# Keys of the second attention held in a zero-filled tile of four row blocks per sequence

## The chip, the cores and the metric

The kernel runs on one NeuronCore of a Trainium2 chip. The metric is device time in microseconds (us): three runs of the kernel before took 1682.60, 1684.46 and 1688.49, median 1684.46. In the profile the core's engines are PE (TensorE's matmuls) with PEld (its weight loads), DVE (VectorE), ACT (ScalarE), POOL (GpSimd) and SP (SyncE, here the issuer of DMAs).

## The reference, cut to what matters

Two decoder layers on `x` of 32 sequences x 128 positions x 256 features, in f32: six sublayers, each added to `x`. The change lies in the fifth, the second layer's cross attention:

```python
def _L1_xattn_ref(q, k, v, Wq, bq, Wk, bk, Wv, bv):
    NUM_HEADS = 16
    B, S, D = q.shape                     # 32, 128, 256
    H, hd = NUM_HEADS, D // NUM_HEADS     # 16, 16
    qp = (q @ Wq + bq).reshape(B, H, S, hd)
    kp = k @ Wk + bk                      # one set of keys for all heads
    vp = v @ Wv + bv
    att = jnp.einsum('bhsd,btd->bhst', qp, kp) / math.sqrt(D)
    att = jax.nn.softmax(att, axis=-1)
    out = jnp.einsum('bhst,btd->bhsd', att, vp)
    return out.transpose(0, 2, 1, 3).reshape(B, S, D)
```

Here `q` is the layer-normed `x`, `k` and `v` are `ctx_1024`. Each of the 16 heads has only 16 features, and all heads of a sequence share the same 128 keys.

## The kernel before

**Stages.** The sublayers run one after another: A (first attention, to about 200 us), B (retention-like cross attention, to about 560), C (experts, to about 1010), D (the rotation sublayer), E (the attention above), F (routed experts, to the end). Stage B also makes the keys and values of stage E, for all groups, and keeps them in SBUF. D, E and the routing of F are interleaved: `stage_e` works in steps `b`, one sequence per step, from b = -13 to 32. E's own scores run from 1138 to 1468 us of the profile.

**Layout.** Sequences come in 8 groups of 4 (`GB = 4`). `kp[g]` has 128 rows and 4 x 128 columns. Its rows are four equal copies (row blocks of 32) of the same keys: 16 rows of key features, one row of ones, 15 rows of zeros. The queries `qT` are 128 rows (four heads of 32 rows: 16 features and 16 zeros) x 4 blocks `j` x 4 sequences x 128 queries. So head 4j + r is block j, row block r.

**Two scores.** The softmax needs the maximum of each query's scores, along the free axis, and then the exponentials with keys on the partitions, for the product with the values. The scores are therefore computed twice:

- `largest` (L1468): for each block j and row block r, queries as weights, keys as moving data, 32 rows, 128 x 128 out. 16 matmuls a sequence. They fill four PSUM banks, one per r, with j inside the bank. Four reductions on DVE (L1475), one per bank, write minus the maximum into a padded tile, `e_pad`.
- `less` (L1481, L1483): four transposes of `e_pad` and an addition on DVE put minus the maximum into the queries' free row, opposite the keys' row of ones. The result is `e_qm`.
- `scores` (L1490): keys as weights, `e_qm` as moving data, 32 rows x 512 columns, one matmul per row block r, each into its own bank. ACT takes the exponential of each bank (L1491).
- `values` (L1498) and `back` (L1508 to L1520): product with the values, transposes, division by the sum, and the addition to `x` on POOL.

**Order.** PE's instructions run in the order in which they are written (`manual_schedule`). In step b it is: `largest` of sequence b+1; `queries` and `turn` of a coming group (L1450, L239); parts of D's rotation (L1296, L1332, L1354) and of F's routing (L156, L354, L355, L611, L629, L633); `values` of b-1; `scores` of b; `back` of b-1; `less` of b+1. The other engines' orders, SP's too, are set by a scheduler. [...]

**Buffers.** PSUM is eight banks: four with the tag "s" (both scores) and four with the tag "m" (all else). `e_hT` (normed, transposed input of a group) and `e_qm` have two buffers each.

**SP in this stage.** Before the change, SP issues here D's writes of `d_line` (L1224), its reads of `d_om` (L1284, in `Turned`, one a group), and, once D's tiles are free, the weights of F's experts (L1628, two loads of 1 MB and a small one). After them come the reads of F's expert blocks (L441).

Of the kernel before, what the change touches and what calls it, by code (L numbers as in the profile page):

```python
# [22 lines left out]
F32 = mybir.dt.float32  # L23
I32 = mybir.dt.int32
AF = mybir.ActivationFunctionType
ALU = mybir.AluOpType
AX = mybir.AxisListType

P = 128
B = 32  # L30
D = 256
NC = D // P
GB = 4
NG = B // GB
GT = GB * P
H = 16
HD = 16
# [3 lines left out]
OM = 64  # L41
# [450 lines left out]
class Route:  # L492


    name = "c"
# [48 lines left out]
class RouteF(Route):  # L544


    name = "f"
# [729 lines left out]
class Turned:  # L1277


    def __init__(self, lie, g, pool):  # L1280
        self.lie, self.k, self.nc, self.g, self.pool = lie, lie.k, lie.nc, g, pool
        self.om = self.full("om")
        half, first = divmod(g * GB, B // 2)
        self.nc.sync.dma_start(out=self.om[0:OM], in_=lie.line[half][first : first + GB].rearrange("b i j -> i b j"))  # L1284

    def tile(self, shape, name, **kw):
        return self.pool.tile(shape, F32, name=f"d_{name}", **kw)
# [123 lines left out]
def stage_e(k, lie, p1, dram, right, halves):  # L1411


    nc, tc = k.nc, k.tc
    J = R = 4
    with (
# [6 lines left out]
        for i in range(2):  # L1423
            t = p1.tile([P, H, 2 * HD], F32, name=f"e_pad{i}")
            nc.gpsimd.memset(t, 0.0)
            pads.append(t)

        k.cf = p1.tile([P, NG, GB, 32], F32, name="f_cf")
        nc.gpsimd.memset(k.cf, 0.0)
        nc.gpsimd.memset(k.cf[:, :, :, E : E + 1], 1.0)  # L1430

        class Group:


            def __init__(self, g):
                self.g = g
                self.stats = k.stats(g)
                self.hT = p2.tile([P, NC, GT], F32, name="e_hT")
                self.qT = p2.tile([P, J, GB, P], F32, name="e_qT")

            def norm(self, behind=None):
# [5 lines left out]
            def queries(self, j, first=0, n=GB):  # L1447
# [7 lines left out]
                    self.qT[:, j, first : first + n], pq, AF.Identity, bias=k.col("E_bq", j)  # L1455
                )

        class Seq:
            def __init__(self, group, i):
                self.group, self.g, self.i = group, group.g, i  # L1460
                self.keys = k.kp[group.g][:, i * P : (i + 1) * P]

            def largest(self):
                ps = [k.bank([P, J, P], "s") for _ in range(R)]
                for j in range(J):
                    for r in range(R):
                        rows = slice(32 * r, 32 * r + 32)
                        nc.tensor.matmul(  # L1468
                            ps[r][:, j, :], lhsT=self.group.qT[rows, j, self.i, :], rhs=self.keys[rows, :],
                            start=True, stop=True,  # L1470
                        )
                self.pad = pads[self.i % 2]
                slots = self.pad.rearrange("p (j r) d -> p j r d", r=R)
                for r in range(R):
                    nc.vector.tensor_reduce(slots[:, :, r, HD], ps[r], AX.X, ALU.max, negate=True)  # L1475

            def less(self):
                pm = k.bank([P, J, P])
                flat = self.pad.rearrange("p m d -> p (m d)")
                for j in range(J):  # L1480
                    nc.tensor.transpose(pm[:, j, :], flat[:, j * P : (j + 1) * P], k.ident)  # L1481
                self.qm = p2.tile([P, J, P], F32, name="e_qm")
                self.less_by = nc.vector.tensor_add(self.qm, pm, self.group.qT[:, :, self.i, :]).ins  # L1483

            def scores(self):
                self.e = p2.tile([P, R, J, P], F32, name="e_e")
                for r in range(R):
                    rows = slice(32 * r, 32 * r + 32)
                    ps = k.bank([P, J, P], "s")
                    nc.tensor.matmul(ps, lhsT=self.keys[rows, :], rhs=self.qm[rows], start=True, stop=True)  # L1490
                    self.exp_by = nc.scalar.activation(self.e[:, r], ps, AF.Exp, scale=1.0 / 16.0).ins  # L1491

            def values(self):
# [28 lines left out]
        with tc.manual_schedule(engines={mybir.EngineType.PE}):  # L1522
            groups, seqs, routes, turned = {}, {}, {}, {}

            def seq(b):
                if 0 <= b < B and b not in seqs:
                    seqs[b] = Seq(groups[b // GB], b % GB)
                return seqs.get(b)

            def step(b, rest=iter(())):  # L1530
                g, i = divmod(b, GB)
                before, this, nxt = seq(b - 1), seq(b), seq(b + 1)

                def due(of, n):

                    lag, rest = divmod(b - n, GB)
                    return of.get(lag) if rest == 0 else None

                route = lambda n: due(routes, n)
                if nxt:  # L1540
                    nxt.largest()
                for n in (-4, -3):
                    if q := due(groups, n):
                        if q.g:
                            for j in range(2 * n + 8, 2 * n + 10):
                                q.queries(j)
                        else:
                            for j in range(J):
                                q.queries(j, 2 * n + 8, 2)
                if q := due(groups, -5):  # L1550
                    q.turn()
                for n, what in ((-9, "add"), (-10, "spin"), (-11, "cube"), (-12, "head"), (-12, "square")):
                    if t := due(turned, n):
                        getattr(t, what)()
                next(rest, None)
                for n, half in ((9, 0), (10, 1)):
                    if r := route(n):
                        r.choose(half)
                if r := route(7):
                    r.turn()  # L1560

                if g == NG - 1:
                    r = routes[i // 2]
                    if i % 2 == 0:
                        r.hidden()
                        r.turn_shares()
                    else:
                        r.shared()
                if before:
                    before.values()  # L1570
                if r := route(12):
                    r.place()
                if this:
                    this.scores()
                if before:
                    before.back()
                if nxt:
                    nxt.less()


                less_by = nxt.less_by if nxt else None
                exp_by = this.exp_by if this else None
                if b >= 5 and i == 1:
                    routes[g - 1] = RouteF(k, g - 1, halves[(g - 1) * 2 // NG], pf, less_by)
                if i == 3 and g + 4 < NG:
                    turned[g + 4] = Turned(lie, g + 4, pd)
                    turned[g + 4].norm(exp_by)
                if i == 1 and 0 <= g + 2 < NG:
                    groups[g + 2] = Group(g + 2)
                if q := due(groups, -6):  # L1590
                    q.norm(exp_by)
                if r := route(6):
                    r.norm(exp_by)
                if r := route(11):
                    r.rank(less_by)
                if r := route(12):
                    r.share(less_by)
                lag, rest = divmod(b - 13, GB)
                if lag in routes:
                    last = routes[lag].store(rest, before.summed)  # L1600
                    if rest == 0:
                        routes[lag].root(last)
                if b == B - 5:
                    halves[0].finish()

            with tc.tile_pool(name="dw", bufs=1, side="right") as pool:
                lie.operands(pd)
                rest = stage_d(k, lie, pool, dram, p2)
                for b in range(-13, -1):
                    step(b, rest)  # L1610
            pf = right.enter_context(tc.tile_pool(name="f1", bufs=2, side="right"))
            for b in range(-1, B + 1):
                if b == B - 12:

                    turns.close()
                    experts = Experts(k, right.enter_context(tc.tile_pool(name="f2", bufs=1, side="right")))
                step(b)
# [185 lines left out]
def sublayers(ctx, k):  # L1803
# [35 lines left out]
    halves = [Dispatch(k, f"g{n}", n * B // 2, B // 2, p1, p2) for n in range(2)]  # L1839
    right = ctx.enter_context(ExitStack())  # L1840
    stage_f(k, *stage_e(k, lie, e1, pd, right, halves), halves)


# [125 lines left out]
```

## Time and profile before

| | us |
|---|---|
| median of three runs | 1684.46 |
| profiled execution, whole | 1686.57 |
| profiled execution, span | 1684.5 |
| PE busy in the span | 1483.5 |
| PEld busy | 982.6 |
| DVE busy | 930.6 |
| ACT busy | 605.6 |
| POOL busy | 601.8 |

How to read the profile: a row of a group names line, engine, operation, the tiles it writes and reads, the shapes and the number of instructions; then busy time in us and the mean length of one instruction in ns; then how long the engine sat idle just before such instructions and what ended that wait. The length of a matmul is its latency: matmuls are pipelined, so the group's busy time and the distance between starts tell the cost. PE's clock is granted in shares of full speed; the mean over the span is 0.926. Stage E's rows in the page:

```profile
L1475 DVE TENSOR_REDUCE e_pad<-ps 128x4 f32<-128x512 f32 x128 | 82.4, 683 | 13.6 <-PE ps L1468 8.9
L1491 ACT ACTIVATE e_e<-ps 128x512 f32<-128x512 f32 x128 | 67.3, 604 | 28.4 <-PE ps L1490 28.3
```

### The profile page before, as it was taken

How to read it: one execution, taken by the hardware profiler on the slowest of the kernel's cores; microseconds unless marked ns; L12 is line 12 of the kernel's file. 1: busy time of each engine (PE TensorE's matmuls, PEld its weight loads, DVE VectorE, ACT ScalarE, POOL GpSimd, SP SyncE). 2: the span in 40 equal slices, each digit the busy share in tenths (PEclk: the TensorE clock that was granted, in tenths of full speed). 3: DMA queues.
4: the chain of work that ended last, by engine and by line, in shares of the span. 5: the costliest groups of instructions: out<-in, count | busy, mean ns of one | idle time of the engine just before them, and what ended most of it. 6: DMA issues, size and time to landing. Idle time of an engine off the chain costs nothing.

```text
span 1684.5 us, 26942 instructions
## 1 busy us (share of the span) xinstructions
PE 1483.5 (88%) x9233; PEld 982.6 (58%) x9233; DVE 930.6 (55%) x3005; ACT 605.6 (36%) x1542; POOL 601.8 (36%) x621
## 2 busy tenths in 40 slices
PE   6999799999997499999999995799999998878873
PEld 3555577776675356666666664445555554556662
DVE  7565446777777533333333324546667766554575
ACT  2444333333333022222222221156665554433331
POOL 2111036577768611111111113122324433365552
PEclk9999999999999589999999995789999988788997
DMA  9990299911002821111111108000000110043486
GB/s 336 336 336 27 68 305 305 254 40 36 24 27 97 330 59 47 47 45 45 48 48 45 45 22 317 12 6 6 3 2 20 66 37 26 26 129 111 141 271 221
DMA packets 133257, 183.85 MB, mean 109 GB/s; under 512 B 12059, under 2 KB 113253, under 8 KB 131077
## 3 DMA queue, kind: packets, MB, share of 16 engines
q1 hardware_dynamic: 116500, 142.28, 27.4%
q0 software_dynamic: 13296, 36.52, 5.9%
q10 hardware_dynamic: 3328, 3.33, 0.6%
q8 instruction: 77, 1.26, 0.3%
q14 instruction: 56, 0.45, 0.1%
HBM read 69.80 MB, written 112.30 MB: 108 GB/s over the span
## 4 chain that ended last, share of the span: by engine, by line
PE 70%; DVE 12%; issue 5%; ACT 5%; POOL 4%; DMA 3%; another core or an unknown queue 1%; POOLq 0%; SPq 0%; ACTq 0%; DVEq 0%
PE ps L1066 13%; PE ps L1086 7%; PE ps L156 6%; PE ps L664 3%; PE ps L1490 2%; PE ps L1450 2%; PE ps L1468 2%; PE ps L1674 2%; PE ps L1690 2%; PE ps L881 2%; PE ps L239 2%; PE ps L1079 2%; PE ps L151 2%; PE ps L897 2%; PE ps L840 1%
## 5 line engine op out<-in xcount | busy, mean ns | idle before, releaser
L1066 PE MATMUL ps<-c_up,c_xT 128*128 x568 | 269.0, 597 | 0.0
L342 POOL DMA_INDIRECT r_ys<-c_yb,r_toi x71 | 68.1, 959 | 354.1 <-DVE r_w L460 313.8
L1066 PEld LDWEIGHTS ps<-c_up,c_xT 128*128 128x128 f32 x568 | 103.2, 192 | 74.0 <-issue 69.7
L1086 PE MATMUL ps<-c_down,c_hid 128*128 x568 | 134.8, 380 | 0.9 <-DVE c_hid L1081 0.9
L1086 PEld LDWEIGHTS ps<-c_down,c_hid 128*128 128x128 f32 x568 | 107.4, 190 | 47.2 <-issue 17.9
L887 DVE TENSOR_TENSOR b_sim<-ps,b_decay 128x512 f32<-128x512 f32 x128 | 79.6, 683 | 83.6 <-PE ps L881 50.9
L146 POOL TENSOR_TENSOR b_rs<-b_var,mhalf 128x16 f32<-128x16 f32 x32 | 93.5, 2922 | 83.8 <-DVE b_var L915 80.7
L1091 ACT ACTIVATE c_yb<-ps,r_w 128x256 f32<-128x256 f32 x71 | 33.6, 473 | 219.0 <-PE ps L1086 219.0
L1081 DVE COPY c_hid<-ps 128x512 f32<-128x512 f32 x71 | 49.1, 691 | 101.5 <-PE ps L1079 101.5
L342 POOL DMA_INDIRECT g_ys<-f_yb,g_toi x78 | 75.7, 971 | 65.0 <-DVE g_to L447 49.3
L1475 DVE TENSOR_REDUCE e_pad<-ps 128x4 f32<-128x512 f32 x128 | 82.4, 683 | 13.6 <-PE ps L1468 8.9
L146 POOL TENSOR_TENSOR ln_rs<-ln_ve,mhalf 128x4 f32<-128x4 f32 x40 | 40.6, 1020 | 128.6 <-DVE ln_ve L175 128.5
L1520 POOL TENSOR_TENSOR x<-x,e_t 128x256 f32<-128x256 f32 x32 | 23.2, 725 | 161.0 <-DVE e_t L1515 161.0
L173 DVE BATCH_NORM_STATS2 ln_st<-x 128x6 f32<-128x256 f32 x192 | 75.0, 407 | 10.1 <-DMA x<-in_x_dram 5.3
L1074 DVE TENSOR_TENSOR c_su<-ps,c_su 128x512 f32<-128x512 f32 x71 | 49.1, 692 | 55.5 <-PE ps L1066 55.5
L1491 ACT ACTIVATE e_e<-ps 128x512 f32<-128x512 f32 x128 | 67.3, 604 | 28.4 <-PE ps L1490 28.3
L1072 ACT ACTIVATE c_su<-ps 128x512 f32<-128x512 f32 x71 | 42.4, 597 | 87.6 <-PE ps L1066 87.6
L342 POOL DMA_INDIRECT r_xs<-c_h,r_rowi x64 | 63.9, 998 | 23.1 <-issue 13.6
L342 POOL DMA_INDIRECT g_xs<-f_h,g_rowi x64 | 62.9, 983 | 23.6 <-issue 16.0
L1468 PE MATMUL ps<-kp,e_qT 32*128 32x128 f32 x1024 | 67.0, 308 | 1.6 <-ACT e_e L1491 1.0
L1690 PE MATMUL ps<-f_rw,f_hb 128*128 x156 | 51.9, 417 | 13.5 <-ACT f_hb L1686 10.0
L1674 PE MATMUL ps<-f_rw,f_xT 128*128 x312 | 53.5, 299 | 11.6 <-ACT f_xT L1666 8.2
(385 smaller groups left out, 3318.4 us busy)
## 6 DMA issues: line engine op xcount, KB each, us to landing
g_xs<-r_empty SPq DMA_DIRECT2D x16, 2193.0 KB
r_xs<-r_empty SPq DMA_DIRECT2D x8, 4290.0 KB
f_xb<-g_xs SPq DMA_DIRECT2D x78, 129.0 KB
c_xb<-r_xs SPq DMA_DIRECT2D x71, 130.0 KB
c_up<-in_wxu_dram SPq DMA_DIRECT2D x4, 2048.0 KB
c_yg<-r_ys SPq DMA_DIRECT2D x8, 1024.0 KB
f_yg<-g_ys SPq DMA_DIRECT2D x16, 512.0 KB
x<-in_x_dram SPq DMA_DIRECT2D x8, 512.0 KB
```

The costliest lines, as they stand in the source:

```text
L146: inst = self.nc.gpsimd.tensor_tensor(out, in_, self.mhalf[: in_.shape[0], 0:n], ALU.pow)
L156: self.nc.tensor.matmul(out, lhsT=(xT[c] if isinstance(xT, tuple) else xT[:, c])[:, i * P : (i + 1) * P], rhs=w(c), start=c == 0, stop=c = ...
L173: self.order(nc.vector.bn_stats(st[:, i, :], x[:, i, :]).ins, behind)
L342: inst = self.nc.gpsimd.indirect_dma_start(out=table, out_offset=bass.IndirectOffsetOnAxis(ap=rows, axis=0), in_=src, in_offset=None,).ins
L887: nc.vector.tensor_mul(self.sim[:, r].rearrange("p c s t -> p (c s t)"), ps[r].rearrange("p c s t -> p (c s t)"), decay[:, r].rearrange("p ...
L1066: nc.tensor.matmul(pu, lhsT=self.xT[:, c, :], rhs=weights(self.j, glu.up[2 * c + u]), start=c == 0, stop=c == NC - 1,)
L1086: nc.tensor.matmul(py, lhsT=self.hid[:, f, :], rhs=weights(self.j, glu.down[f]), start=f == 0, stop=f == NF0 - 1,)
L1468: nc.tensor.matmul(ps[r][:, j, :], lhsT=self.group.qT[rows, j, self.i, :], rhs=self.keys[rows, :], start=True, stop=True,)
L1475: nc.vector.tensor_reduce(slots[:, :, r, HD], ps[r], AX.X, ALU.max, negate=True)
L1491: self.exp_by = nc.scalar.activation(self.e[:, r], ps, AF.Exp, scale=1.0 / 16.0).ins
L1674: nc.tensor.matmul(pu, lhsT=self.xT[:, c, :], rhs=experts.rw1[:, self.at, c, :].rearrange("p n f -> p (n f)"), start=c == 0, stop=c == NC - 1,
L1690: nc.tensor.matmul(po, lhsT=self.hid, rhs=experts.rw2[:, self.at, :].rearrange("p n f -> p (n f)"), start=True, stop=True,)
```

## The change

Three tiles `e_keys` of 128 rows x 4 x 128 columns are filled with zeros once. For each sequence, four DMAs copy row block r of `kp` into rows 32r to 32r+31 of column block r: the keys stand in the four diagonal blocks, all else stays zero. A sequence takes the tile of its number modulo 3; the copies for sequence b+2 are issued in step b.

In `largest`, one matmul per block j takes all 128 rows of `qT` as weights and the whole tile, 512 columns, as moving data. Each bank now holds one j with the four r inside, and the reductions go by j. In `scores`, column block r of the tile is the weights: 128 rows, of which 32 are keys and the others zero, so the moving data is all of `e_qm`. PSUM banks, reductions and exponentials keep their number and size.

`e_hT` and `e_qm` go from two buffers to one. The first three tiles' copies are put behind the first read of `d_om` in SP's order.

```diff
@@ class Turned
-        self.nc.sync.dma_start(out=self.om[0:OM], in_=lie.line[half][first : first + GB].rearrange("b i j -> i b j"))
+        self.fetched = self.nc.sync.dma_start(
+            out=self.om[0:OM], in_=lie.line[half][first : first + GB].rearrange("b i j -> i b j")
+        ).ins
@@ stage_e
+        spread = []
+        for i in range(3):
+            t = p2.tile([P, R, P], F32, name=f"e_keys{i}", bufs=1)
+            nc.vector.memset(t, 0.0)
+            spread.append(t)
+
@@ class Group
-                self.hT = p2.tile([P, NC, GT], F32, name="e_hT")
+                self.hT = p2.tile([P, NC, GT], F32, name="e_hT", bufs=1)
@@
+        def spread_keys(b):
+
+            g, i = divmod(b, GB)
+            for r in range(R):
+                rows = slice(32 * r, 32 * r + 32)
+                load = nc.sync.dma_start(out=spread[b % 3][rows, r, :], in_=k.kp[g][rows, i * P : (i + 1) * P])
+                if b < 3:
+                    k.order(load.ins, turned[0].fetched)
+
@@ class Seq
-                self.keys = k.kp[group.g][:, i * P : (i + 1) * P]
+                self.keys = spread[(GB * group.g + i) % 3]

             def largest(self):
-                ps = [k.bank([P, J, P], "s") for _ in range(R)]
-                for j in range(J):
-                    for r in range(R):
-                        rows = slice(32 * r, 32 * r + 32)
-                        nc.tensor.matmul(
-                            ps[r][:, j, :], lhsT=self.group.qT[rows, j, self.i, :], rhs=self.keys[rows, :],
-                            start=True, stop=True,
-                        )
                 self.pad = pads[self.i % 2]
                 slots = self.pad.rearrange("p (j r) d -> p j r d", r=R)
-                for r in range(R):
-                    nc.vector.tensor_reduce(slots[:, :, r, HD], ps[r], AX.X, ALU.max, negate=True)
+                ps = [k.bank([P, R, P], "s") for _ in range(J)]
+                for j in range(J):
+                    nc.tensor.matmul(
+                        ps[j], lhsT=self.group.qT[:, j, self.i, :], rhs=self.keys, start=True, stop=True
+                    )
+                for j in range(J):
+                    nc.vector.tensor_reduce(slots[:, j, :, HD], ps[j], AX.X, ALU.max, negate=True)

             def less(self):
...
-                self.qm = p2.tile([P, J, P], F32, name="e_qm")
+                self.qm = p2.tile([P, J, P], F32, name="e_qm", bufs=1)
...
             def scores(self):
                 self.e = p2.tile([P, R, J, P], F32, name="e_e")
                 for r in range(R):
-                    rows = slice(32 * r, 32 * r + 32)
                     ps = k.bank([P, J, P], "s")
-                    nc.tensor.matmul(ps, lhsT=self.keys[rows, :], rhs=self.qm[rows], start=True, stop=True)
+                    nc.tensor.matmul(ps, lhsT=self.keys[:, r, :], rhs=self.qm, start=True, stop=True)
                     self.exp_by = nc.scalar.activation(self.e[:, r], ps, AF.Exp, scale=1.0 / 16.0).ins
@@ step
                 if b == B - 5:
                     halves[0].finish()
+                if 0 <= b + 2 < B:
+                    spread_keys(b + 2)
```

## The prediction

> **What bounds the kernel now.** I read the page's busy row first, then the windows over the stretch in which the second attention runs, then the groups by shape for the two scores, then the timeline of one step.
>
> The table of windows (columns: stretch, its length, busy time with instruction count of PE, PEld, DVE, ACT, POOL, then granted clock, DMA share, GB/s):
>
> ```profile
> 1150.00:1190.00 40.00, 39.17 (x325) 22.43 (x327) 27.05 (x60) 25.14 (x50) 10.10 (x13) 1.00 0.01 3
> 1190.00:1230.00 40.00, 38.89 (x308) 23.12 (x303) 25.62 (x63) 23.92 (x50) 9.84 (x12) 0.96 0.01 2
> 1230.00:1270.00 40.00, 38.27 (x313) 23.14 (x312) 28.41 (x93) 23.74 (x51) 9.84 (x12) 1.00 0.01 2
> 1270.00:1310.00 40.00, 38.30 (x290) 22.79 (x292) 28.85 (x94) 23.58 (x50) 17.30 (x21) 0.96 0.06 21
> 1310.00:1350.00 40.00, 37.26 (x290) 21.80 (x291) 28.32 (x97) 20.03 (x44) 19.04 (x23) 0.95 0.22 80
> 1350.00:1390.00 40.00, 38.95 (x292) 23.64 (x294) 26.51 (x95) 21.10 (x41) 15.79 (x19) 0.88 0.08 28
> 1390.00:1430.00 40.00, 33.70 (x254) 19.25 (x253) 24.51 (x99) 15.30 (x28) 13.38 (x16) 0.83 0.08 27
> 1430.00:1480.00 50.00, 43.27 (x255) 26.05 (x253) 27.77 (x115) 21.99 (x37) 19.41 (x23) 0.80 0.11 35
> ```
>
> PE has 93 to 98% of its time filled up to 1390, DVE at most 72%, ACT 63%, and the DMA engines are nearly empty. So PE sets the pace of this stage, and its order of instructions is written by hand: time added to a matmul group moves the end, unless it falls into one of PE's gaps. From 1150 to 1480 these gaps are 0.8+1.1+1.7+1.7+2.7+1.1+6.3+6.7 = 22 us.
>
> The groups by shape (busy time, mean ns of one; then PE's idle time before the group and who ended it):
>
> ```profile
> L1468 PE MATMUL ps<-kp,e_qT 32*128 32x128 f32 x1024 | 67.0, 308 | 1.6 <-ACT e_e L1491 1.0 <-ACT d_rows L1223 0.3
> L1490 PE MATMUL ps<-e_qm,kp 32*128 32x512 f32 x256 | 53.7, 696 | 5.5 <-DVE e_pad L1475 5.5
> L1450 PE MATMUL ps<-e_hT,w_wE 128*128 128x512 f32 x112 | 51.8, 605 | 0.0
> ```
>
> L1468 is the first score (for the maximum), L1490 the second. 32 sequences times 16 matmuls are 512, the row has 1024: an f32 matmul is two instructions. The mean of 308 or 696 ns is latency; four row blocks run at once, so the cost is the busy time: 67.0/32 = 2.1 us and 53.7/32 = 1.7 us a sequence. L1450 is the row that stands for the new matmuls: all 128 rows, 512 columns, f32.
>
> One step in the timeline (start, length, engine, line):
>
> ```profile
> 1252.52 1.14 PE L1490 MATMUL ps<-e_qm,kp 32*128 32x512 f32 x8
> 1253.59 0.66 PE L1508 MATMUL ps<-ident,e_oT 128*128 128x128 f32 x4
> ...
> 1254.09 0.60 PE L1481 MATMUL ps<-ident,e_pad 128*128 128x128 f32 x4
> ...
> 1254.62 2.48 PE L1468 MATMUL ps<-kp,e_qT 32*128 32x128 f32 x32
> ...
> 1257.02 3.70 PE L1450 MATMUL ps<-e_hT,w_wE 128*128 128x512 f32 x8
> ...
> 1260.56 0.60 PE L1332 MATMUL ps<-ident,d_y 128*64 128x128 f32 x4
> ```
>
> Eight packed instructions of L1490 let the next group start after 1.07 us; eight full-array ones of L1450 after 3.54 us. That is the whole case. L1468 takes 2.40 us here because its banks wait for the exponentials (its weight loads sit idle for ACT's L1491, 11.7 us over the stage); without that wait it takes 1.10 us (at 1246.29).
>
> **The change part by part.**
>
> *First score.* Removed: 16 matmuls a sequence (32 instructions). Added: 4 of 128x512 (8 instructions).
>
> *Second score.* 4 matmuls of 32x512 become 4 of 128x512: 8 instructions either way, but each on all rows, so no two run at once.
>
> New in all: 32 x (8+8) = 512 instructions. Price from L1450: 3.54/8 = 0.443 us in the step shown, 3.63/8 = 0.454 in the next step (1269.45 to 1273.08), 51.8/112 = 0.463 as the stage's mean, cold stretches included. I take 0.45: 230 us, with ends 227 and 237. Old: 67.0 + 53.7 = 120.7, less the 0.07 us by which each of the 64 groups' modelled ends overlaps the next start (1252.52+1.14 against 1253.59), 4.5: 116 us. Difference **+114**.
>
> *The rule on packing.* The Trainium skill, "TensorE: Matmul & The Clock Gate", section "Part 3: Packing small matmuls", says that a matmul on 32 rows takes as long as one on 128, and that four of them in different row groups run together, 3.07 times as fast as in turn. It speaks against this change. By it alone a packed score costs 3.6/3.07 = 1.17 us (3.6 = 8 x 0.45) and the change 64 x (3.6 - 1.17) = +155. The rows price the old scores higher, 116/64 = 1.8 us, since they count the waits on PSUM banks inside the groups. The measured rows decide: +114. "TensorEngine Tiling (Array Packing)", "Key Properties", speaks for the change: a new tiling mode drains the array, and the old step changes mode around both scores. If it cost much, a gap would stand there; but L1481's four transposes start 0.53 us before L1468, 0.13 each, with no gap. I take nothing for it.
>
> *Waits inside and before the scores.* Idle before L1490 and L1468, 5.5 + 1.6 us: four banks used to fill together at the end of the first score, so four reductions of 0.68 us (L1475) queued behind it. Now bank j is ready every 0.9 us and its reduction runs beside the next matmul. **-7**. What is late next is PE itself.
>
> *The other gaps.* 22 - 7 = 15 us, mostly PE waiting for DVE's routing work (2.63 before L611 at 1423.66, 1.55 before L355 at 1346.56). DVE's work doesn't grow and each step has 3.6 us more, so much is covered; 2.93 before L239 at 1458.62, a step without a next sequence, is not. Between 0 and -15: **-7**.
>
> *Clock.* The granted share falls below 1 in the windows above: 40 x (0.04+0.04+0.05+0.12+0.17) + 50 x 0.20 = 27 us of clock lost, in patches behind gaps. Fewer gaps, fewer patches; but a full-array score in a cold patch costs 8 x 0.9 = 7 us where the packed one took 3.9 (1406.45), waits included. From -12 to +10, no row tells; nearer to the few gaps that go: **-4**.
>
> *DMAs of the keys.* 4 a sequence, 128 in all, on SP. No row shows one of 32 rows; the nearest issue is d_om's (L1284), 0.57 to 0.63 us, so at most 2.5 us of SP per step of 10, and SP is otherwise waiting. They wait for the second score of sequence b-1, in step b-1, land some 2.2 us later (d_om's on the chain at 1194.79), and are wanted at the start of step b+1. A whole step covers them: nothing. Without cover it would be 2 to 3 us a step. On SP they stand behind the om loads, whose wait (the cube of an earlier group) ends in or before the same step, and in front of none that is short. One place is tight: the last quarter of sequence 22's keys is queued behind the expert weights of L1628. Before, these are issued at 1341.06, 10.6 us after L1354 of the same step, and 2 MB are through by 1350 (192 then 281 GB/s in two windows of 5 us). So the keys land some 22 us after that L1354; PE wants them 20.6 us after it (1351.05) plus what three heavier scores add, 3 to 5 us. Between 0 and +5; I take 0.
>
> *The rest, at nothing.* Three memsets of 128x512 on DVE (at most 0.7 us each, like DVE's 128x512 copies) fall in 1000 to 1040, where DVE is busy 18.6 of 40 us and stage D waits for scattered rows; uncovered they cost 2. One buffer for e_hT: the next write (turn) comes two steps after the last read (queries) in PE's own order. One for e_qm: its add waits for L1481, which PE runs after the scores that read the old one. The reductions have the same count and size, the exponentials too. Ends: 0 to +2.
>
> **Sum.** 114 - 7 - 7 - 4 = +96 on the profiled execution, whose span is 1684.5 (1686.6 with what lies around it, 2 above the median of the runs). On the median: 1684.5 + 96 = **1780**.
>
> **Rivals.** (1) *Keys late*: PE waits each step for the four DMAs, say 3 us by 32: about 1875. For it: SP takes them in order and the loads chain on completions. Against: a whole step of lead and empty DMA engines. (2) *Slack swallows half*: if DVE's chains, not PE, end most steps (DVE is at 70%), all gaps close and the clock stays at 1 throughout: 114 - 22 - 27 = +65, 1750. Against: only 22 us of gaps exist. (3) *Faster*: dense full-row work holds the clock at 1 and removes every bank wait, so that the stage comes out ahead, at 1675. It decides once the new instruction costs less than (116+22+27)/512 = 0.32 us; L1450 at full clock shows 0.44. I see no room for it. That it doesn't do what it says is excluded: PE's order in the built kernel has 12 matmuls a sequence fewer and is otherwise unchanged.
>
> **How the numbers follow.** Forecast 0.81, keys late 0.05 (a part of this, a few us, is in the range), half swallowed 0.12, faster 0.015, no change 0.005. Range: low 227-116-7-15-12 = +77, high 237-116-7+0+5 = +119 (237 has cold stretches in it already), and 3 more either way for part of the rivals: 1758 to 1806. No change means within 0.3%, 5 us, about what can be told apart here.
>
> **What would show it.** After: two groups of 256 full-row matmuls with some 115 us of busy time each in place of 67.0 and 53.7; PE at 97% or more in the stage; no idle before the second score; the attention's stretch from 1138 to 1468 longer by 90 to 100. Key DMAs as a releaser of PE in each step would prove rival 1. The forecast is wrong if the full-row matmuls take well under 0.44 us, or if the clock's share in the stage moves by more than 0.1.

## The result, and the profile after

The changed kernel takes 1751.24 us (median of six runs, 1750.66 to 1752.39) against 1685.70 for the kernel before beside it: ratio 1.038, 95% interval 1.0365 to 1.0394, slower by 65.5 us. The forecast of 1780 had the sign and the largest term, but the time lies 7 us below its range.

The groups of the page that answer to L1468, L1490, L1450, L1475 and L1491 (columns as before):

```profile
L1503 PE MATMUL ps<-e_qm,e_keys 128*128 128x512 f32 x256 | 118.3, 605 | 0.0
L1485 PE MATMUL ps<-e_keys,e_qT 128*128 128x512 f32 x256 | 115.3, 593 | 0.0
...
L1489 DVE TENSOR_REDUCE e_pad<-ps 128x4 f32<-128x512 f32 x128 | 86.4, 685 | 8.8 <-PE ps L1485 8.5
L1504 ACT ACTIVATE e_e<-ps 128x512 f32<-128x512 f32 x128 | 75.8, 598 | 33.6 <-PE ps L1503 33.1
```

The scores' busy time went from 120.7 to 233.6 us, and PE no longer waits before either. The same answer by shapes gives the neighbour:

```profile
L1458 PE MATMUL ps<-e_hT,w_wE 128*128 128x512 f32 x112 | 50.3, 592 | 0.0
```

The windows of the stage, in the columns shown for the kernel before (the column before the last two is the granted clock):

```profile
1160.00:1200.00 40.00, 40.00 (x155) 19.63 (x154) 19.43 (x35) 18.81 (x38) 7.10 (x9) 1.00 0.03 8
1240.00:1280.00 40.00, 40.00 (x168) 20.33 (x166) 19.12 (x53) 16.10 (x29) 7.20 (x9) 1.00 0.02 6
1320.00:1360.00 40.00, 40.00 (x168) 21.08 (x167) 26.59 (x84) 21.09 (x44) 18.96 (x23) 1.00 0.08 27
1400.00:1440.00 40.00, 40.00 (x162) 19.89 (x162) 20.00 (x73) 19.88 (x37) 12.43 (x15) 1.00 0.17 62
1480.00:1520.00 40.00, 39.83 (x166) 20.03 (x165) 26.32 (x118) 17.33 (x28) 11.50 (x15) 1.00 0.08 28
```

This is the surprise: PE is filled to the last hundredth and its clock stands at 1.00 to the end of the stage, where the kernel before had 0.77 to 0.91. From the first score to the last transposes the stage takes 395.7 us instead of 334.2. So 61.5 of the 65.9 us by which the span grew lie here, and the rest of the kernel is nearly as before.

PE's waits in the stage, all that are left (who waited for whom, us in total, times, longest):

```profile
PE ps L239 <- ACT f_h L190: 1.0, 4, 0.5
PE ps L1511 <- ACT e_e L1504: 0.2, 1, 0.2
PE ps L1521 <- ACT e_oT L1516: 0.2, 1, 0.2
PE ps L355 <- DVE g_cum L338: 0.2, 1, 0.2
```

No DMA stands among them: the keys are in time in every step.

**Where the forecast's 96 became 66.** Four entries, each summed from the two traces over the stage. Where the modelled ends of two groups overlap, the time is counted once, to the matmul that started last, so the entries add up to the stage:

| term | forecast | measured |
|---|---|---|
| 512 new instructions | 230 | 223.7 |
| packed scores removed | -116 | -116.4 |
| PE's idle time in the stage | -14 | -21.0 (22.6 to 1.6) |
| PE's other groups in the stage | -4 (clock) | -24.8 (195.2 to 170.4) |
| sum | +96 | +61.5 |

The other 4 us lie outside the stage, most of them in stage F.

The last entry has two parts. Of the clock that the kernel before lost in the stage, 14.8 us fall into these other groups; in the changed kernel nothing is lost. For the rest, the timeline shows where most of it lies. At full clock, a step of the changed kernel, from the run e5 that repeated it on another chip (columns: start, duration, engine, line, operation):

```profile
1311.01 3.70 PE L1503 MATMUL ps<-e_qm,e_keys 128*128 128x512 f32 x8
1314.55 0.60 PE L1521 MATMUL ps<-ident,e_oT 128*128 128x128 f32 x4
1314.98 0.60 PE L1495 MATMUL ps<-ident,e_pad 128*128 128x128 f32 x4
1315.42 3.60 PE L1485 MATMUL ps<-e_keys,e_qT 128*128 128x512 f32 x8
```

The two groups of four transposes take 0.43 and 0.44 us from start to start. Before, between packed scores, they took 0.50 and 0.53 (1253.59, 1254.09, 1254.62). That is 0.16 us a sequence, 5 us in all, for the switches between 32 and 128 rows. Some 3 us more are gone from L1450 and L239, which also stood behind a packed score; the last 2 us are spread over small groups.

### The profile page after: what moved, and what is told of

Its sections match the earlier page's. It is cut to its first block, busy times and chain, and to the rows that moved or that the text cites. A ratio compares the mean times of both kernels' runs of the same rounds, so it can differ in the third digit from the quotient of the medians.

```text
span 1750.4 us, 25748 instructions
## 1 busy us (share of the span) xinstructions
PE 1568.4 (90%) x8465; PEld 1002.8 (57%) x8465; DVE 935.3 (53%) x3008; ACT 616.5 (35%) x1542; POOL 605.2 (35%) x621
## 4 chain that ended last, share of the span: by engine, by line
PE 78%; DVE 8%; issue 5%; POOL 3%; DMA 3%; ACT 2%; another core or an unknown queue 0%; SPq 0%; POOLq 0%; ACTq 0%; DVEq 0%
PE ps L1066 13%; PE ps L1503 6%; PE ps L1086 6%; PE ps L1485 6%; PE ps L156 6%; PE ps L664 3%; PE ps L1458 3%; PE ps L1689 2%; PE ps L1705 2%; PE ps L239 2%; PE ps L881 2%; PE ps L1511 2%; PE ps L151 2%; PE ps L1079 2%; PE ps L897 2%
## 5 line engine op out<-in xcount | busy, mean ns | idle before, releaser
L1503 PE MATMUL ps<-e_qm,e_keys 128*128 128x512 f32 x256 | 118.3, 605 | 0.0
L1485 PE MATMUL ps<-e_keys,e_qT 128*128 128x512 f32 x256 | 115.3, 593 | 0.0
L1489 DVE TENSOR_REDUCE e_pad<-ps 128x4 f32<-128x512 f32 x128 | 86.4, 685 | 8.8 <-PE ps L1485 8.5
L1504 ACT ACTIVATE e_e<-ps 128x512 f32<-128x512 f32 x128 | 75.8, 598 | 33.6 <-PE ps L1503 33.1
L1503 PEld LDWEIGHTS ps<-e_qm,e_keys 128*128 128x128 f32 x256 | 46.0, 190 | 67.8 <-issue 50.2
L1485 PEld LDWEIGHTS ps<-e_keys,e_qT 128*128 128x128 f32 x256 | 46.1, 190 | 46.8 <-issue 40.5
L342 POOL DMA_INDIRECT r_xs<-c_h,r_rowi x64 | 64.3, 1005 | 22.8 <-issue 13.8
```

What stands on the lines that cost most here:

```text
L342: inst = self.nc.gpsimd.indirect_dma_start(out=table, out_offset=bass.IndirectOffsetOnAxis(ap=rows, axis=0), in_=src, in_offset=None,).ins
L1485: nc.tensor.matmul(ps[j], lhsT=self.group.qT[:, j, self.i, :], rhs=self.keys, start=True, stop=True)
L1489: nc.vector.tensor_reduce(slots[:, j, :, HD], ps[j], AX.X, ALU.max, negate=True)
L1503: nc.tensor.matmul(ps, lhsT=self.keys[:, r, :], rhs=self.qm, start=True, stop=True)
```

## The experiments

All runs but the first comparison were on four other chips, on each of which the kernel before takes 1644 to 1647 us. Its profile on one of them (e15) has the same stage, 330.5 us long, with gaps and lost clock as expected; of the 40 us between the two profiles 33 are missing in stage F, 179 us instead of 212. Differences in us below are against the kernel before on the same chip. "Gaps" and "lost clock" of a run are summed over the stage, from the first score to the last transposes: the time that PE is not busy, and (1 - granted clock) x length. They come from one profiled execution each. Stages that are alike differ in lost clock by up to 7 us (e11 and e13), so less than that is not read.

| run | against before, us | gaps | lost clock |
|---|---|---|---|
| before (first chip / e15) | 0 | 22.6 / 21.0 | 25.9 / 22.2 |
| e5 changed kernel again | +65.3 | 1.6 | 0.0 |
| e9 change without key loads | +66.7 | 1.6 | 0.0 |
| e1 first score only | +7.7 | 10.9 | 5.1 |
| e2 second score only | +29.9 | 22.8 | 8.5 |
| e3 packed twice | +80.2 | 34.7 | 33.0 |
| e4 filler, 128 rows | +27.6 | 21.8 | 15.4 |
| e7 filler, 32 rows | +28.5 | 20.4 | 27.3 |
| e6 change, 32 rows | +257 | 1.1 | 175.8 |
| e10 change, 64 rows | +90 | 1.1 | 10.2 |
| e8 first score later | +23.7 | 34.2 | 38.8 |
| e11 shift on POOL | +1.4 | 17.6 | 15.4 |
| e12 e1 with that shift | +18.5 | 11.0 | 3.4 |
| e13 shift on POOL, stage E only | -6.9 | 17.9 | 22.4 |
| e14 the same, placement later | -11.1 | 13.4 | 24.4 |

### One score at a time (e1, e2)

```diff
 e1, scores:
-                    nc.tensor.matmul(ps, lhsT=self.keys[:, r, :], rhs=self.qm, start=True, stop=True)
+                    rows = slice(32 * r, 32 * r + 32)
+                    nc.tensor.matmul(ps, lhsT=self.packed[rows, :], rhs=self.qm[rows], start=True, stop=True)
```

e2 is the mirror: `largest` as before, from `kp`, and `scores` from the tile.

> Only the first score uses the zero-filled tile; the second is packed, from kp, as before. PE gets 115 - 65 = 50 us more matmul time. Theory 'gaps' (the change's extra PE time is first swallowed by the stage's 22 us of PE gaps and 27 us of lost clock, and only the rest shows): +5 to +25 us against before, the stage's clock near 1. Theory 'sum' (most of the extra time shows, as forecast): +40 to +48, the clock as before.

> Only the second score uses the zero-filled tile; the first is packed, from kp, as before. PE gets 118 - 51 = 67 us more. Theory 'gaps': +18 to +40, clock near 1, and this run and the one of the first score alone together give less than the +66 of the whole change, since both draw on the same slack. Theory 'sum': +55 to +65.

Measured: 1.0043 (1.0028 to 1.0057) and 1.0184 (1.0167 to 1.0201). Both as "gaps" had it, and 7.7 + 29.9 = 38 is far less than the 65 of both together. The first score's 50 us of added matmul time cost 8 us; the second score, on top of it, costs 58 us for some 70. The slack is shared and finite. The packed partner gets cheaper too: a full-array score hands over its banks one by one. In e2 (groups by shape):

```profile
L1507 PE MATMUL ps<-e_qm,e_keys 128*128 128x512 f32 x256 | 121.1, 617 | 10.9 <-DVE e_pad L1493 10.9
...
L1488 PE MATMUL ps<-kp,e_qT 32*128 32x128 f32 x1024 | 38.4, 283 | 0.3 <-ACT d_rows L1223 0.3
```

The packed first score takes 38.4 us here against 67.0: the waits for ACT inside it are gone. But the gap ahead of the second score stays, since the packed first score still fills four banks at once.

### Added work of two kinds (e3, e4, e7)

```diff
 e3, both scores (in scores the exponentials come after both rounds):
+                for _ in range(2):
                     for j in range(J):
 e4, both scores (scores alike; e7: rows 0:32 of both operands):
+                nc.tensor.matmul(ps[0], lhsT=self.group.qT[:, 0, self.i, :], rhs=k.kp[self.g], start=True, stop=True)
                 for j in range(J):
```

> The kernel before, each packed score computed twice in the same banks: 64 x 1.07 = 68 us more PE time, all of it on 32-row tiles. Theory 'gaps' (the clock falls only behind gaps of PE, and any added work closes them): clock of the stage 0.97 or more, +18 to +35 us. Theory 'rows' (32-row matmuls don't hold the clock up, matmuls on all rows do): the clock stays near 0.92 and the time rises by 45 to 60.

> The kernel before with one surplus matmul of 128x512 on all rows ahead of each packed score, in the score's own first bank: 64 x 0.9 = 58 us more PE time. Both theories, gaps and rows: clock near 1, +8 to +22 us. Theory 'sum': +45 or more.

> The twin of the filler run with all rows: the same surplus matmul of 512 columns ahead of each packed score, but on rows 0 to 31 only. Theory 'gaps': the same as its twin, +22 to +32 us, clock lost in the stage 13 to 18 us. Theory 'rows': more clock lost, 25 us or more, and +35 us or more.

e3 missed both forecasts: +80 us for 68 us of work. Its row gives a part of the reason:

```profile
L1492 PE MATMUL ps<-e_qm,kp 32*128 32x512 f32 x512 | 88.9, 685 | 15.7 <-DVE e_pad L1476 15.7
```

The repetition makes the banks ready later, all at once, so DVE starts later and PE waits 15.7 us before the second score instead of 5.5. Packed work did not bring the clock back either: 33 us lost.

e4 was above its range (+27.6), as it closed hardly any gap. e4 and e7 have the same columns in the same place, and gaps alike. With 32 rows the clock lost is 27 us, with 128 it is 15, as "rows" had it; the time is nevertheless the same (+28.5 and +27.6), so "rows" missed there. The timelines show where most of the 12 us went. In e4 the filler (L1492) stands ahead of the packed score; in e7 the score's other row blocks start beside it, and the two take 1.91 us (1253.37 to 1255.28) instead of 2.13 (1258.22 to 1260.35). In the medians of both scores that is 0.3 us a sequence, 10 us in all:

```profile
1258.22 1.12 PE L1492 MATMUL ps<-e_qm,kp 128*128 128x512 f32 x2
1259.28 1.14 PE L1493 MATMUL ps<-e_qm,kp 32*128 32x512 f32 x8
1260.35 0.66 PE L1511 MATMUL ps<-ident,e_oT 128*128 128x128 f32 x4
...
1253.37 0.69 PE L1492 MATMUL ps<-e_qm,kp 32*128 32x512 f32 x1
1253.39 0.70 PE L1493 MATMUL ps<-e_qm,kp 32*128 32x512 f32 x3
...
1255.28 0.66 PE L1511 MATMUL ps<-ident,e_oT 128*128 128x128 f32 x4
```

### Rows or gaps (e6, e10)

```diff
-                        ps[j], lhsT=self.group.qT[:, j, self.i, :], rhs=self.keys, start=True, stop=True
+                        ps[j], lhsT=self.group.qT[0:32, j, self.i, :], rhs=self.keys[0:32], start=True, stop=True
-                    nc.tensor.matmul(ps, lhsT=self.keys[:, r, :], rhs=self.qm, start=True, stop=True)
+                    nc.tensor.matmul(ps, lhsT=self.keys[0:32, r, :], rhs=self.qm[0:32], start=True, stop=True)
```

e10 has 64 in place of 32.

> The changed kernel with both scores on rows 0 to 31 only: as many matmuls, each of 512 columns, but with a quarter of the rows driven. This leaves out the heads of row blocks 1 to 3. Theory 'gaps': PE stays filled, so the clock stays at 1.00 and the time is that of the changed kernel within 8 us (a few us more if weight loads into the same row block can't run ahead). Theory 'rows': with PE filled all the same, the clock falls to 0.90 or below for much of the stage and the time is 15 us or more above the changed kernel.

> The changed kernel with both scores on rows 0 to 63; this leaves out the heads of row blocks 2 and 3. If the clock follows the rows that a matmul drives, step by step: PE filled, clock of the stage between 0.72 (32 rows) and 1.00 (128 rows), time between those two runs. If there is a threshold below which activity doesn't count: the clock is either at 1.00 or as low as with 32 rows.

e6, windows, the last of them the whole stage:

```profile
1160.00:1200.00 40.00, 40.00 (x91) 16.71 (x90) 10.64 (x19) 10.02 (x18) 1.45 (x2) 0.60 0.02 5
1240.00:1280.00 40.00, 40.00 (x129) 18.66 (x126) 20.63 (x51) 19.03 (x40) 9.10 (x11) 0.83 0.01 3
1400.00:1440.00 40.00, 40.00 (x116) 19.57 (x115) 16.73 (x48) 18.10 (x38) 9.77 (x11) 0.70 0.04 15
...
1134.00:1715.70 581.70, 580.56 (x1602) 266.79 (x1602) 231.32 (x714) 190.54 (x363) 111.94 (x135) 0.70 0.04 15
```

PE has hardly a gap (1.1 us in 582), and yet the mean clock is 0.70. The 176 us of lost clock are most of the 192 by which e6 is slower than the changed kernel. The timeline shows a cold score of eight instructions at 7.19 us, twice the 3.6 of the changed kernel:

```profile
1398.93 7.19 PE L1503 MATMUL ps<-e_qm,e_keys 32*128 32x512 f32 x8
1406.05 1.12 PE L1521 MATMUL ps<-ident,e_oT 128*128 128x128 f32 x4
1406.96 1.06 PE L1495 MATMUL ps<-ident,e_pad 128*128 128x128 f32 x4
```

So the theory that only gaps pull the clock down falls: a busy PE that drives 32 rows loses it by itself. One thing fell together with the rows: of the four weights of a second score, three hold only zeros in e6 and two in e10. Whether the clock follows the rows or the data in them was not separated. With 64 rows almost all of it is back (10 us lost, in one stretch from 1480), which looks like a threshold and not like a share. e10's +25 us over the changed kernel (two executions) is more than its lost clock. About 0.3 us a sequence, 11 us in all, are the switches of row form: from L1503 to the end of L1485 it takes 8.28 us (1317.83 to 1326.11), where the changed kernel takes 7.94 (1311.01 to 1318.95).

### The changed kernel again, and without key loads (e5, e9)

```diff
 e9:
-                if 0 <= b + 2 < B:
+                if 0 <= b + 2 < 3:
```

> The changed kernel unaltered, as the reference on this chip for the next runs. Both theories: +60 to +70 us against before, the stage's clock at 1.00 and PE without gaps.

> The changed kernel without the key DMAs after the first three sequences: it leaves out 116 of the 128 loads, so later sequences score against stale keys. If the loads are hidden a whole step ahead: within 3 us of the changed kernel, that is +60 to +70 us against before. If PE waits for keys in steps: 10 us or more below the changed kernel.

e5: 1.0402 (1.0378 to 1.0426); the change costs the same on a chip with another stage F. e9: 1.0401 (1.0364 to 1.0438), 66.7 us above before. It gains nothing without the later loads, so the DMAs of the keys cost nothing that shows.

### Cheaper packed scores (e8, e11 to e14)

e8 moves `nxt.largest()` behind `queries` and `turn` in `step`. e11 moves the layer norm's shift, e12 is e1 with e11, e13 keeps the last shift on DVE, e14 adds a move of `r.place()` behind `before.back()`:

```diff
 e11:
-        self.nc.vector.scalar_tensor_tensor(nb, mv[:, :, 0], -1.0, rs, ALU.mult, ALU.mult)
+        self.nc.gpsimd.tensor_tensor(nb, mv[:, :, 0], rs, ALU.mult)
+        self.nc.gpsimd.tensor_tensor(nb, nb, self.minus, ALU.mult)
```

> The kernel before with one move in PE's order: the packed first score comes after the coming group's queries and transposes instead of ahead of them, so that its banks are free when it starts. If the 47 us of bank waits inside the two packed scores are real and lie on PE's path: -8 to -25 us against before. If DVE's reductions then end later and the second score waits as much: within 5 us of before.

> The kernel before with the layer norm's shift (L183, a 128x4 operation that waits in DVE's queue for POOL's root, ahead of the reductions) computed on POOL instead. Theory: the gaps it causes (3.7 us before L1490, up to 10.7 us of DVE waits in the stage) go, and with each the cold patch behind it: -5 to -15 us against before. Rival: DVE is late for other reasons: within 3 us.

> The first score alone on the zero-filled tile, with the shift on POOL as well. That kernel was 8 us above before with 11 us of gaps and 5 us of lost clock left in the stage: -4 to +6 us against before; at the low end it would be the better of all kernels but the one with the shift alone.

> As the run with the shift on POOL, but the last group's routing in stage F keeps it on DVE. There the stage of the second attention was 10 us shorter (322 against 332 us from its first reduction to its last transposes) and nothing of it reached the end, stage F being 185 us instead of 180. Theory (POOL's queue of scatters delayed that last shift): -4 to -10 us against before. Rival (F doesn't start earlier for another reason): within 3 us.

> The same, and the routing's placement (L354, L355), at which PE waited 4.7 us for DVE's running sums, moved behind the packed second score. Theory 'a gap starts a cold patch': with these gaps gone too, about 10 us of gaps and under 10 us of lost clock are left in a stage whose scores are still packed; -8 to -18 us against before. If packed scores by themselves hold the clock down, the clock lost stays at 15 us or more and the time gains 5 us or less on the run with the shift alone.

> The kernel before, unaltered, for its profile on this chip: the stage 330 to 334 us long, 20 to 24 us of gaps and 22 to 28 us of lost clock in it, as in the profile already shown.

e8 is slower, 1.0158 (1.0125 to 1.0191), which neither theory had: the wait inside the first score falls (48.7 us instead of 67.0), but the reductions end later and PE waits for them before the second score, 12.0 us instead of 5.5.

e11, 1.0009 (0.9993 to 1.0025), missed its theory and lies in its rival's range, though not for the rival's reason: its stage is shorter, but stage F grew to 184 us. e12, 1.0115 (1.0087 to 1.0143), missed; its stage F is 188. e13 returns it: 0.9956 (0.9941 to 0.9971).

e14: 0.9945 (0.9925 to 0.9966), 1635.8 us, the lowest median of all kernels here, below before and the change. In its profile the gaps fell to 13.4 us and the lost clock didn't fall (24.4). But this profile is of an execution of 1644.99 us, 9 above the median. Over all executions, e14's median clock is 0.936 against 0.9305 for the kernel before beside it. From these two shares I estimate 9 us less lost clock over the whole span. So e14 doesn't settle whether closing gaps brings the clock back while the scores are packed.

Its trace does show where such loss starts without a gap. A stretch at half clock, from 1262.1 to 1268.9, has 0.01 us of gaps in the 10 us ahead of it (two windows, then PE):

```profile
1251.80:1262.10 10.30, 10.29 (x65) 5.00 (x64) 9.92 (x31) 6.59 (x13) 4.02 (x5) 1.00 0.00 1
1262.10:1268.90 6.80, 6.80 (x48) 5.15 (x48) 4.60 (x24) 0.90 (x3) 0.72 (x1) 0.50 0.01 2
...
1259.12 3.10 PE L1496 MATMUL ps<-e_qm,kp 32*128 32x512 f32 x8
1262.16 1.12 PE L1514 MATMUL ps<-ident,e_oT 128*128 128x128 f32 x4
```

The packed score ahead of it takes 3.04 us instead of 1.07: its blocks wait for banks and start 0.6 to 0.7 us apart, one after the other. The latency of each fills the wait, so it counts as busy. The other two such stretches of e14 (1361.1 and 1398.7) also stand behind a drawn-out packed score. So waits inside the groups are a rival to "packed scores drive too few rows", and no run separates the two.

## Why the prediction was right or wrong

**What bounds, and the direction: right.** PE paces the stage, and most of the full-array scores' time shows. e1 refines it: the first score's 50 us are nearly free.

**Price of the new instructions: 6 us too high.** I took 0.45 us from L1450's distances between starts, with room for cold stretches; the scores ran at 0.43 to 0.44 (3.44 to 3.54 us for eight), and the clock was never low.

**Old scores and their bank waits: right.** 116 us, and the idle time before both went to zero.

**The rule on packing: right as a warning, wrong as a sum.** Packed scores do take about 1.1 us without waits, but the waits belong to them; the rows of the profile decided rightly. That 32 rows take as long as 128 (the page has this under "Why this matters for your kernels") holds here: eight such instructions took 3.63 us at full clock in e6. **The rule on switching modes: wrongly set to nothing.** I read 0.53 us for four transposes as "no gap"; with all groups on 128 rows the same four take 0.44. That is 5 us for the transposes, and up to 10 with all groups beside packed scores.

**The other gaps: 7 us too few.** All of them closed, not half. By the waits that are left, the added PE time lets DVE and ACT finish in each step.

**The clock: the step that failed most, by 11 us.** I tied the lost clock to gaps, took -4 on the reasoning that only few gaps go, and wrote that no row tells. In the changed kernel the clock stays at 1.00, and the other groups get back 14.8 us. e6 shows that closing the gaps is not enough for that: with 1 us of gaps 32-row scores lose 176 us of clock, 64-row ones 10 (e10), 128-row ones none (e5). So the scores hold the clock up, and every other group of the stage runs at full clock. The Trainium skill ties the clock to how busy PE is ("TensorE: Matmul & The Clock Gate", "Part 1: The HAM clock gate"); e6 adds that busy isn't enough. Why the packed kernel loses its 22 to 26 us stays open: at like gaps e2, with only the second score on all rows, loses 9, but there the waits inside the packed first score are gone too.

**DMAs of the keys, the memsets, the single buffers: right, at nothing.** The three memsets took 0.49 us each. e9 excludes rival 1. Even the quarter behind the expert weights, issued at 1396.02, made PE wait for nothing.

**Rival 2 gave the time (1750), in part by luck.** All gaps closed and the clock stayed at 1, as it says; but not because DVE's chains ended the steps. It also takes off all 27 us of lost clock, though 9 of them lay inside the packed scores, which the 116 already count; the switches of row form and the cheaper new instruction, which it lacks, made up for that. I held against it that there are only 22 us of gaps, and overlooked the clock. It deserved more than 0.12. Rival 3 failed by its own measure: the new instruction took 0.44 us, not 0.32.

## What to carry to other kernels

Before costing added work on an engine that is 95% busy, add up that engine's gaps and the clock lost in the groups that stay, and ask what share the new work takes back: here 46 of 107 us, 10 of them from switches of row form. Zero-padding small matmuls to all rows gives up their concurrency, and still cost only 8 us for one of two scores, where PSUM banks came free one by one and the clock lost fell to 5 us. When a packed kernel shows a low granted clock, look at the rows that it drives and at waits inside its groups, and not at its idle time alone.

## What the runs showed of the hardware

- A busy PE is not enough for a full granted clock: 0.70 over the stage at 580.56 of 581.70 us busy with 32 rows (e6), 1.00 with 128 rows (e5), and 10 us lost with 64 (e10). Whether four packed blocks at once count like one block was not tried by itself.
- A switch between matmuls of 64 and 128 rows costs about 0.1 us at each edge (0.34 us for the four edges of two scores, e10 against e5), although no idle time shows between the groups.
- The same kernel took 1685 us on one chip and 1644 to 1647 on four others. The stage studied here was alike on the first and on the one profiled for it (334.2 and 330.5 us); most of the difference lies in stage F and was not pursued.
